# Reordering the projection steps of the later attention batches: begun half a unit sooner, the values' correction in two row tiles, the last diagonal ahead of its search

## The chip, the core and the metric

The kernel runs on one core of a Trainium2 chip, in float32. The core has four engines that compute: TensorE (PE; its weight loads are listed apart as PEld), VectorE (DVE), ScalarE (ACT) and GpSimd (POOL). SyncE (SP), ACT and POOL also issue DMA transfers between HBM and the on-chip SBUF. TensorE writes only into PSUM, whose eight banks are shared among the tiles below. The metric is device time in microseconds (us), the median of the runs shown; lower is better.

## The reference: what is computed

Eight batches of 1024 tokens with 512 features pass through a "macaron" block: half a feed-forward network, an attention, and half a feed-forward network again.

```python
x = x + 0.5 * ffn(layernorm(x))
x = x + attention(layernorm(x))
x = x + 0.5 * ffn(layernorm(x))
```

`ffn` is a mixture of 32 experts, each of which chooses tokens. A gate gives logits per token and expert, softmax runs over the tokens, and each expert takes its eight best tokens of a batch, merges them with their probabilities into one row, sends that row through a 512-2048-512 network with GELU, and adds the result back to the eight tokens. `attention` is a causal linear attention with 16 heads of 32 features: q = exp(x Wq + bq), k = exp(x Wk + bk), and

```python
kv  = cumsum(k[:, :, :, None] * v[:, :, None, :], axis=1)
k1  = cumsum(k, axis=1)
out = einsum('zsD,zsDd->zsd', q, kv) / sum(q * k1, -1)
```

## The kernel before

**Stages.** The kernel first routes all tokens, then runs the experts of the first FFN (`experts(0, ...)`), the attention, the experts of the second FFN, and a last scatter. The experts' weights are 268 MB in each FFN, so these stages stream weights. Beside the first FFN, TensorE has time to spare, and `speculate` uses it: for batches 4 to 7 it centres x, projects it to q, k and v (without the first FFN's contribution, which isn't known yet and has rank 32) and stores the result in HBM as `ahead_d`.

**Units and chunks.** The attention handles a batch as eight chunks `c` of 128 tokens; two chunks make a unit `u` (U = 2, UT = 256 columns). Each unit needs q, k, the running sum k1 of k, and the values `va`. For batches 0 to 3 `project` makes them with full matmuls. For batches 4 to 7 (`NB0 = 4`) `project_rest` loads `ahead_d` as `pre` and corrects it by rank 32, with `pm` (the routing probabilities) times `oW` (the experts' outputs times the weights). The tile `pm4` holds `pm` of the batch four times, once in each block of 32 partitions. The steps of `project_rest` are:

- L631: add the output bias to x on POOL. L636 to L650: spread the reciprocal deviations over the partitions (`rsb`), scale `pm` to `pmr` and scale the q and k part of `pre`, on POOL. Issue the load of the next unit's `pre` (L652). Then two bare yields.
- L663: eight correction matmuls for q and k (`ps_qk`), into both `sp` tiles. L672: two additions on DVE. L675: eight exps on ACT.
- L678: `sum_keys`, four scans on DVE (L709).
- L684: two matmuls for the values' correction (`ps_v`), both from the same 32 rows, each listed as two records. L688: two DVE steps that make `va`.
- L697: `times_keys`, qk = q * k1 on POOL (L720).

**A chunk of the attention.** `scores` (L766) multiplies k by q into the two `sp` tiles; DVE masks one half into `am` (L777), ACT copies the other (L782) and POOL masks it (L784). `denominators`, in the even chunk, sums q * k1 (`ps_den`, L728) and inverts it on DVE (`rd`, L736); `spread_denominators` repeats it (L747, L754). `turn_keys` transposes k (L816, copy L818). `attend` multiplies `am` by `va` (`ps_n`, L830), adds the state's part (L842), divides (`at`, L851) and updates the state (L862, L871). `project_out` multiplies by Wo (L880), adds to x (L887) and takes moments for the next routing (L314). The generator `begin` of the next batch (`begun`) scatters the first FFN's output into x (L293, L300, L308) and takes moments. The generator `route` (`gate`) makes the routing for the second FFN: the gate's scale (L380 to L399), `choose` (the searches L407, L412 and L414, the softmax L416 to L424), the diagonal `diag` (L512), `ps_pmT` (L519), `ps_m` (L539), `ps_mT` (L562).

**What sets the order.** `attention` is a loop over batches and chunks that calls these functions and advances the generators with `next`. The order of the calls is the program order. The instructions are then put in each engine's queue by the framework's planner: it plays the program with its own durations and gives each engine the ready instruction that comes first in program order, so the queue can differ from program order. An engine runs its queue in order. `tc.keep_in_program_order` pins an instruction behind the one before it on its engine. In an odd chunk of the kernel before, the order of calls is: a step of `begun`, `scores`, a step of `ahead` (the bare yield), `turn_keys`, `project_out` of the chunk before, a step of `ahead` (L656 to L697, all of it), a step of `gate`, `attend`. PSUM: `mm` has three banks in turn (`ps_o`, `ps_n`, `ps_v`, `ps_kt`, `ps_den`, `ps_sc` and others), `sp0` and `sp1` take two banks each and serve `scores`, `ps_qk` and the spread denominators in turn, and `sum` holds the state.

**The last routing.** For batch 7 `route` gets a tile `el` and runs without pauses behind the last chunk. Its scale is done in groups of 4, 2, 1 and 1 chunks. `choose` then pins the index search (L427) behind the reciprocal (L424), and `diag` (L512) follows both on DVE.

Of the kernel before, what the change touches and what calls it, by code (L numbers as in the profile page):

```python
# [8 lines left out]
F32 = mybir.dt.float32  # L9
# [6 lines left out]
P = 128  # L16
# [4 lines left out]
def kernel(  # L21
# [52 lines left out]
    nc = tc.nc  # L74
    B, S, D = x_in.shape
    E = w1.shape[0]
    FF = w1.shape[2]
    NCH = S // P
# [3 lines left out]
    U = 2  # L82
# [3 lines left out]
    NB0 = 4  # L86
# [285 lines left out]
    def gate_scale(t, s, b, lg, rs, at, k):  # L372


        own = slice(32 * (b % 4), 32 * (b % 4) + E)
        raw = s["raw", b]
        pr = t.mm.tile([NCH, P], F32, tag="mm", name=f"ps_rsT_{b}_{at}")
        nc.tensor.transpose(pr[:k, :], rs[:, at : at + k], ident)
        rsT = t.p2.tile([NCH, P], F32, tag="rsT", name=f"rsT_{b}_{at}")
        nc.scalar.copy(rsT[:k, :], pr[:k, :])  # L380
        yield
        halves = range(at // 4, (at + k - 1) // 4 + 1)
        c0, n = at % 4, min(k, 4)
        rows = slice(E * c0, E * (c0 + n))
        ps = t.mm.tile([P, 2, P], F32, tag="mm", name=f"ps_rs_{b}_{at}")
        for i, h in enumerate(halves):
            nc.tensor.matmul(
                ps[rows, h, :],
                lhsT=pick8[:k, i, :n, :].rearrange("k c e -> k (c e)"),
                rhs=rsT[:k, :],  # L390
                start=True,
                stop=True,
            )
        hs = slice(halves[0], halves[-1] + 1)
        nc.vector.tensor_mul(raw[rows, hs, :], raw[rows, hs, :], ps[rows, hs, :])
        to = lg.rearrange("p (h c s) -> p c h s", h=2, c=4)
        for c in range(c0, c0 + n):
            r = slice(E * c, E * (c + 1))
            nc.scalar.activation(  # L399
                to[own, c, hs, :], raw[r, hs, :], AF.Identity, bias=gb_sb[r]  # L400
            )

    def choose(t, lg, rows, g, name, listed=False, el=None):


        top = t.p2.tile([P, 8], F32, tag="top", name=f"top_{name}")
        nc.vector.max(top[rows, :], lg[rows, :])  # L407
        pinned = el is not None
        sm = t.p2.tile([P, 3], F32, tag="sm", name=f"sm_{name}")
        nc.vector.tensor_scalar_mul(sm[rows, 0:1], top[rows, 0:1], -1.0)  # L410
        rest = pm[:, g, :]
        nc.vector.match_replace(rest[rows, :], top[rows, :], lg[rows, :], -1.0e30)  # L412
        if listed and not pinned:
            nc.vector.max_index(chosen_idx[rows, g, :], top[rows, :], lg[rows, :])  # L414
        el = el if pinned else lg
        nc.scalar.activation(  # L416
            el[rows, :], lg[rows, :], AF.Exp, bias=sm[rows, 0:1], accum_out=sm[rows, 1:2]
        )
        kept = nc.vector.scalar_tensor_tensor(
            rest[rows, :], rest[rows, :], -0.9e30, el[rows, :], ALU.is_lt, ALU.mult  # L420
        )
        if pinned:
            tc.keep_in_program_order(kept)
        nc.vector.reciprocal(sm[rows, 2:3], sm[rows, 1:2])  # L424
        if pinned:
            tc.keep_in_program_order(
                nc.vector.max_index(chosen_idx[rows, g, :], top[rows, :], lg[rows, :])  # L427
            )
        return rest, sm[rows, 2:3]

    def gather_four(t, xs, rs4, chosen, r, g):
# [49 lines left out]
    def route(t, s, b, el=None):  # L481
# [25 lines left out]
                yield  # L507
        if el is None:
            yield
        chosen, r = choose(t, lg, rows, g, f"b{b}", True, el)  # L510
        diag = t.p2.tile([P, E], F32, tag="diag", name=f"diag_{b}")
        nc.vector.tensor_scalar_mul(diag[rows, :], ident[rows, rows], r)  # L512
        if el is None:
            yield

# [102 lines left out]

    def project_rest(t, s, b, u):

        xt, mv, rs = s["xt", b]
        pre = s.pop(("pre", b, u))
        if u == 0:
# [27 lines left out]
        if (b, u) < (B - 1, NCH // U - 1):  # L651
            load_ahead(t, s, *divmod(b * (NCH // U) + u + 1, NCH // U))  # L652
        yield
        yield

        qkT = open_unit(t, s, b, u)  # L656
        sp = [
# [15 lines left out]
        for n, bias in ((1, bk_sb), (0, bq_sb)):  # L673
            for oc in range(NDC):
                nc.scalar.activation(  # L675
                    qkT[:, oc, n, :], qkT[:, oc, n, :], AF.Exp, bias=bias[:, oc : oc + 1]
                )
        sum_keys(t, s, b, u)  # L678

        r = slice(32 * (b % 4), 32 * (b % 4) + E)  # L680
        for i in range(U):
            c = u * U + i
            ps = t.mm.tile([P, D], F32, tag="mm", name=f"ps_v_{b}_{c}")
            nc.tensor.matmul(  # L684
                ps, lhsT=pmr[r, i * P : (i + 1) * P], rhs=s["oWv"][r, :], start=True, stop=True
            )
            va = t.a2.tile([P, D], F32, tag="va", bufs=3, name=f"va_{b}_{c}")
            nc.vector.scalar_tensor_tensor(  # L688
                va,
                pre[:, (2 * NDC + i * 2) * UT : (2 * NDC + i * 2 + 2) * UT],  # L690
                rs[:, c : c + 1],
                ps,
                ALU.mult,
                ALU.add,
            )
            s["va", b, c] = va
        times_keys(t, s, b, u)  # L697
        yield

# [211 lines left out]
    def outputs_ahead(t, s):  # L911


        ocT = outputs_turned(t, s, NB0 // 4)
        s["oW"] = t.ow.tile([P, B - NB0, 2, P], F32, name="oW")
        for i in range(2):
            ps = t.mm.tile([P, 2, 2, P], F32, tag="mm", name=f"ps_oW{i}")
            for b in range(2):
                r = 32 * ((NB0 + 2 * i + b) % 4)
                for n, w in enumerate("qk"):  # L920
                    for dc in range(NDC):
                        for j in range(4):
                            nc.tensor.matmul(
                                ps[E * j : E * (j + 1), b, n, :],
                                lhsT=ocT[:, dc, r : r + E],
                                rhs=w_sb[w][:, dc, j * P : (j + 1) * P],
                                start=(dc == 0),
                                stop=(dc == NDC - 1),
                            )
            evacuate(s["oW"][:, 2 * i : 2 * i + 2], ps)  # L930
        s["oWv"] = t.ow.tile([P, D], F32, name="oWv")
        ps = t.mm.tile([P, D], F32, tag="mm", name="ps_oWv")
        for dc in range(NDC):
            nc.tensor.matmul(
                ps, lhsT=ocT[:, dc, :], rhs=w_sb["v"][:, dc, :], start=(dc == 0), stop=(dc == NDC - 1)
            )
        evacuate(s["oWv"], ps)

    def attention(t, early, preload):

# [46 lines left out]
        for b in range(B):  # L987
            for c in range(NCH):
                if c == 0:
# [12 lines left out]
                    if b + 1 < B:  # L1002
                        s["loaded", b + 1] = load_x(t.xp, x_in, b + 1, f"xt{(b + 1) % 3}")
                        begun = begin(b + 1)
                if c > 1:
                    next(begun, None)
                if b == B - 1 and c == 1:
                    preload(0)
                if b == B - 1 and c == NCH - 2:
                    late.close()  # L1010
                    preload(1)
                    preload(2)
                    preload(3)
                    el = end.enter_context(tc.tile_pool(name="el", bufs=1, side="right")).tile(
                        [P, S], F32, name="el"
                    )
                    gate = route(t, s, b, el)
                scores(t, s, b, c)
                if c % U == 0:
                    denominators(t, s, b, c // U)  # L1020
                    nb, nu = divmod(b * (NCH // U) + c // U + 1, NCH // U)
                    if (nb, nu) == (NB0, 0):

                        for i in range(2):
                            values(t, s, b, c + i)
                        early.close()
                        t.s1 = late.enter_context(
                            tc.tile_pool(name="s1", bufs=1, side="right", reuse_waits="tile")
                        )
                        t.s2 = late.enter_context(  # L1030
                            tc.tile_pool(name="s2", bufs=2, side="right", reuse_waits="tile")
                        )
                        load_ahead(t, s, nb, nu)
                    if (nb, nu) > (0, 1):
                        of = project if nb < NB0 else project_rest
                        ahead = of(t, s, nb, nu) if nb < B else iter(())
                        next(ahead, None)
                else:
                    next(ahead, None)
                if ("va", b, c) not in s:  # L1040
                    values(t, s, b, c)
                turn_keys(t, s, b, c)
                if last is not None:
                    project_out(t, s, *last)
                    if c == 0:
# [10 lines left out]
                if c % U == 0:  # L1056
                    spread_denominators(t, s, b, c // U)
                else:
                    next(ahead, None)
                next(gate, None)  # L1060
                if (b, c) == (0, 1):
                    outputs_turned(t, s, 0)
                attend(t, s, b, c)
                last = (b, c)
        gate_sums(t, s, B - 1, range(NCH - 2, NCH - 1))
        next(gate)
# [575 lines left out]
```

## Time and profile before

| what | value |
|---|---|
| median of 3 runs (lowest, highest) | 2618.5 us (2616.56, 2619.34) |
| the profiled execution: its time | 2614.58 us |
| its span, from the first to the last instruction | 2612.9 us |
| mean granted TensorE clock | 0.916 |
| busy in the span: PE, PEld, DVE, ACT, POOL | 2176.2, 1153.6, 869.7, 500.6, 376.8 us |
| HBM, mean over the span | 254 GB/s |
| attention: first and last scores of the trace | 859.7 and 1935.9 us |
| L631, of project_rest: first and last | 1398.8 and 1807.6 us |
| first matmul of the second FFN's experts (L1206) | 1971.59 us |

Durations and places in time come from the one profiled execution, counted from the start of its span. The page lists busy times for each engine; a line such as L663 is line 663 of the kernel. In a timeline a row gives start, duration, engine, line, operation, the tiles written and read, and how many instructions it merges; in brackets stands the idle time of the engine before it and what ended that. The row "PEclk" is the clock that TensorE was granted, in tenths.

### The profile page before, as it was taken

The page shows a single profiled execution, that of the slowest core. Times are in us where ns is not written, and L with a number is a line of the kernel's source. Part 1 is how long each engine was busy: PE and PEld are TensorE (multiplying, and loading weights), DVE is VectorE, ACT ScalarE, POOL GpSimd, SP SyncE. Part 2 cuts the span into 40 slices and gives each one's busy share as a digit, 9 for nine tenths or more (in the row PEclk, how much of TensorE's full clock was granted, in tenths as well). Part 3 has the DMA queues.
Part 4 walks back from the last instruction along what each step waited for, and adds up shares of the span by engine and source line. Part 5 has one row for each costly group of instructions (what it writes and reads, how often), then busy time and mean ns, then how long its engine had stood idle before and what let it go on. Part 6 is the DMA issues. An engine that isn't in the chain of part 4 may idle for free.

```text
span 2612.9 us, 41804 instructions
## 1 busy us (share of the span) xinstructions
PE 2176.2 (83%) x18679; PEld 1153.6 (44%) x18679; DVE 869.7 (33%) x1493; ACT 500.6 (19%) x967; POOL 376.8 (14%) x345
## 2 busy tenths in 40 slices
PE   8799999898977999999999989898886555555555
PEld 6354454454533666666666655555541111111111
DVE  7311111111102443544535476767751000100002
ACT  6300001000001322222222243343430000000000
POOL 0000000000000211111122244445324000000002
PEclk9899999999998999999999988999997778878788
DMA  7899999999996000010100323323159999999996
GB/s 278 316 417 428 426 427 427 427 427 427 428 429 234 1 18 11 11 50 19 59 2 19 95 81 132 112 107 108 66 196 377 422 428 428 428 428 427 428 428 255
DMA packets 95476, 667.97 MB, mean 256 GB/s; under 512 B 18222, under 2 KB 22574, under 8 KB 58432
## 3 DMA queue, kind: packets, MB, share of 16 engines
q1 hardware_dynamic: 73792, 621.45, 57.9%
q10 hardware_dynamic: 18432, 35.66, 3.5%
q0 software_dynamic: 3072, 8.19, 0.8%
q8 instruction: 146, 2.39, 0.4%
q14 instruction: 34, 0.28, 0.0%
HBM read 614.34 MB, written 48.23 MB: 254 GB/s over the span
## 4 chain that ended last, share of the span: by engine, by line
PE 49%; issue 23%; DMA 14%; DVE 7%; ACT 1%; POOL 1%; SPq 0%; POOLq 0%; ACTq 0%; DVEq 0%
DMA w<-in_w 10%; PE ps_o L880 8%; PE ps_k L599 4%; PE ps_q L599 4%; PE ps_v L800 4%; PE ps_sk L1116 3%; PE ps_sq L1116 3%; PE p_ps L1229 3%; PE h_ps L1206 3%; PE ps_sv L1133 2%; PE ps_n L830 2%; PE sp L766 2%; PE ps_n L842 2%; DMA xg<-out,chosen_idx 2%; DVE un L709 1%
## 5 line engine op out<-in xcount | busy, mean ns | idle before, releaser
L1206 PE MATMUL h_ps<-w,mT 128*8 128x512 f32 x2048 | 288.6, 698 | 126.7 <-DMA w<-in_w 126.0
L1215 DVE STREAM_TRANSPOSE hs<-h_ps 128x512 f32<-128x512 f32 x64 | 45.9, 717 | 723.7 <-PE h_ps L1206 723.7
L1229 PE MATMUL p_ps<-w,pm 128*32 128x512 f32 x1024 | 172.1, 805 | 132.8 <-DMA w<-in_w 127.8
L880 PE MATMUL ps_o<-wo_sb,at 128*128 128x512 f32 x512 | 236.4, 605 | 1.0 <-DVE at L851 0.8
L1206 PEld LDWEIGHTS h_ps<-w,mT 128*8 128x8 f32 x2048 | 50.4, 95 | 339.7 <-issue 205.0
L1229 PE MATMUL p_ps<-w,gl 128*32 128x512 f32 x1024 | 132.7, 651 | 40.7 <-DMA w<-in_w 40.4
L590 POOL TENSOR_TENSOR xt<-xt,bo_sb 128x512 f32<-128x512 f32 x32 | 45.8, 1447 | 767.0 <-PE ps_ocT L338 706.7
L1229 PEld LDWEIGHTS p_ps<-w,pm 128*32 128x32 f32 x1024 | 35.3, 129 | 270.4 <-issue 134.4
L880 PEld LDWEIGHTS ps_o<-wo_sb,at 128*128 128x128 f32 x512 | 94.1, 194 | 100.7 <-issue 95.9
L784 POOL TENSOR_SCALAR_AFFINE_SELECT am<-am 128x512 f32<-128x512 f32 x128 | 78.7, 639 | 413.7 <-ACT am L782 276.3
L314 DVE BATCH_NORM_STATS2 st<-xt 128x6 f32<-128x512 f32 x192 | 129.4, 686 | 4.1 <-DMA xt<-in_x 1.0
L599 PE MATMUL ps_k<-xnT,wk_sb 128*128 128x256 f32 x512 | 115.3, 383 | 10.8 <-ACT xnT L339 10.8
L1222 ACT ACTIVATE pm<-a 128x128 f32<-128x128 f32 x32 | 9.9, 309 | 586.5 <-DVE a L1217 586.5
L1116 PE MATMUL ps_sq<-xcT,wq_sb 128*128 128x256 f32 x512 | 118.3, 387 | 4.0 <-ACT xcT L241 4.0
L1116 PE MATMUL ps_sk<-xcT,wk_sb 128*128 128x256 f32 x512 | 117.3, 385 | 0.0
L1133 PE MATMUL ps_sv<-wv_sb,xcT 128*128 128x512 f32 x256 | 115.6, 599 | 0.0
L800 PE MATMUL ps_v<-wv_sb,xnT 128*128 128x512 f32 x256 | 115.1, 593 | 0.0
L599 PE MATMUL ps_q<-xnT,wq_sb 128*128 128x256 f32 x512 | 115.1, 382 | 0.0
L1116 PEld LDWEIGHTS ps_sq<-xcT,wq_sb 128*128 128x128 f32 x512 | 96.4, 192 | 34.8 <-issue 17.0
L1116 PEld LDWEIGHTS ps_sk<-xcT,wk_sb 128*128 128x128 f32 x512 | 96.7, 191 | 27.9 <-issue 15.4
L599 PEld LDWEIGHTS ps_k<-xnT,wk_sb 128*128 128x128 f32 x512 | 95.8, 190 | 28.4 <-ACT xnT L339 14.6
L766 PE MATMUL sp<-un 32*128 32x128 f32 x2048 | 100.1, 293 | 7.2 <-ACT un L675 7.0
(245 smaller groups left out, 2888.8 us busy)
## 6 DMA issues: line engine op xcount, KB each, us to landing
w<-in_w SPq DMA_DIRECT2D x256, 2048.0 KB, 29.5
xt<-in_x SPq DMA_DIRECT2D x31, 1024.0 KB, 10.7
pre<-ahead_d SPq DMA_DIRECT2D x16, 1536.0 KB, 6.7
ahead_d<-ahead_qk ACTq DMA_DIRECT2D x16, 1024.0 KB, 11.7
out<-xt SPq DMA_DIRECT2D x16, 1024.0 KB, 4.4
xs<-in_x ACTq DMA_DIRECT2D x16, 512.0 KB, 19.8
ahead_d<-ahead_v ACTq DMA_DIRECT2D x16, 512.0 KB, 11.1
pm<-pm SPq DMA_DIRECT2D x16, 128.0 KB, 2.5
```

The source lines that it names most:

```text
L314: nc.vector.bn_stats(st, xt[:, c, :])
L599: nc.tensor.matmul(ps[:, o, :], lhsT=w_sb[n][:, dc, oc * P : (oc + 1) * P], rhs=xnT[:, dc, :], start=(dc == 0), stop=(dc == NDC - 1),)
L766: nc.tensor.matmul(sp[r // 2][:, r % 2, og, :], lhsT=kT[hr, og, cols], rhs=qT[hr, og, cols], start=True, stop=True,)
L784: nc.gpsimd.affine_select(out=am[1][:, i, :, :], in_=am[1][:, i, :, :], pattern=[[0, NDC], [1, P]], compare_op=ALU.is_ge, fill=0.0, base=0 ...
L800: nc.tensor.matmul(ps, lhsT=s["xnT", b, c // U][:, dc, cols], rhs=w_sb["v"][:, dc, :], start=(dc == 0), stop=(dc == NDC - 1),)
L830: nc.tensor.matmul(ps[hr, og, :], lhsT=va[:, (og * HG + r) * HD : (og * HG + r + 1) * HD], rhs=am[r // 2][:, r % 2, og, :], start=(og == 0 ...
L842: nc.tensor.matmul(ps[hr, og, :], lhsT=kv[hr, og, :], rhs=qT[hr, og, cols], start=False, stop=True, skip_group_check=True,)
L880: nc.tensor.matmul(ps, lhsT=at[:, oc, :], rhs=w_sb["o"][:, oc, :], start=(oc == 0), stop=(oc == NDC - 1),)
L1116: nc.tensor.matmul(ps[:, o, :], lhsT=w_sb[w][:, dc, oc * P : (oc + 1) * P], rhs=xcT[:, dc, :], start=(dc == 0), stop=(dc == NDC - 1),)
L1133: nc.tensor.matmul(ps, lhsT=xcT[:, dc, i * P : (i + 1) * P], rhs=w_sb["v"][:, dc, :], start=(dc == 0), stop=(dc == NDC - 1),)
L1206: nc.tensor.matmul(h[32 * j : 32 * j + B, :], lhsT=mT[:, dc, e, :], rhs=w1h[dc // 2][:, dc % 2, j * 512 : (j + 1) * 512], start=(dc == 0), ...
L1229: nc.tensor.matmul(pp[32 * j : 32 * (j + 1), :], lhsT=gl4[e % 4][:, q, :, :].rearrange("p i b -> p (i b)"), rhs=w2h[q // (NU // 2)][:, q % ...
```

## The change

Six edits, all in the attention.

- `project_rest` is cut into four steps instead of three (one of them bare): (A) up to the next load; (B) `ps_qk`, additions, exps; (C) the values' correction and `va`; (D) `sum_keys` and `times_keys`.
- For units of batches 4 to 7 (`rest`) A still runs in the even chunk behind the denominators. B now runs at the end of the even chunk, behind `attend`. In the odd chunk `turn_keys`, C and a step of `gate` come ahead of `scores`; D comes behind `project_out` and behind the step of `begun`, which in these odd chunks moves there from the head of the chunk.
- The two value matmuls of a unit use two row tiles: chunk i uses the 32 rows of batch b + i (mod 4) of `pmr`, with a second copy of `oWv` that is turned by 32 partitions. That copy is made once, by two DMAs on SP, at the start of the later batches.
- In `choose` with `el`, the index search is no longer issued; `route` scales the diagonal first and then issues the search, both pinned in this order.
- In `gate_scale` the copy of `rsT` is on DVE instead of ACT where a single chunk is handled (`k == 1`, twice, in the last routing).

```diff
-        nc.scalar.copy(rsT[:k, :], pr[:k, :])
+        (nc.vector.tensor_copy if k == 1 else nc.scalar.copy)(rsT[:k, :], pr[:k, :])
...
         if pinned:
-            tc.keep_in_program_order(
-                nc.vector.max_index(chosen_idx[rows, g, :], top[rows, :], lg[rows, :])
-            )
+            return rest, sm[rows, 2:3], top
...
-        chosen, r = choose(t, lg, rows, g, f"b{b}", True, el)
+        chosen, r, *top = choose(t, lg, rows, g, f"b{b}", True, el)
         diag = t.p2.tile([P, E], F32, tag="diag", name=f"diag_{b}")
-        nc.vector.tensor_scalar_mul(diag[rows, :], ident[rows, rows], r)
+        scaled = nc.vector.tensor_scalar_mul(diag[rows, :], ident[rows, rows], r)
+        if el is not None:
+            tc.keep_in_program_order(scaled)
+            tc.keep_in_program_order(
+                nc.vector.max_index(chosen_idx[rows, g, :], top[0][rows, :], lg[rows, :])
+            )
...
             load_ahead(t, s, *divmod(b * (NCH // U) + u + 1, NCH // U))
-        yield
         yield
...
-        sum_keys(t, s, b, u)
-
-        r = slice(32 * (b % 4), 32 * (b % 4) + E)
+        yield
+
+        ps = [t.mm.tile([P, D], F32, tag="mm", name=f"ps_v_{b}_{u * U + i}") for i in range(U)]
+        for i in range(U):
+            r = slice(E * ((b + i) % 4), E * ((b + i) % 4 + 1))
+            nc.tensor.matmul(
+                ps[i],
+                lhsT=pmr[r, i * P : (i + 1) * P],
+                rhs=s["oWv", i][r, :],
+                start=True,
+                stop=True,
+            )
...
             s["va", b, c] = va
+        yield
+        sum_keys(t, s, b, u)
         times_keys(t, s, b, u)
         yield
...
+                nb, nu = divmod(b * (NCH // U) + c // U + 1, NCH // U)
+
+                rest = NB0 <= nb < B
-                if c > 1:
+                if c > 1 and not (rest and c % U):
                     next(begun, None)
...
+                if rest and c % U:
+                    turn_keys(t, s, b, c)
+                    next(ahead)
+                    next(gate, None)
                 scores(t, s, b, c)
...
+                        oWv = s["oWv", 1] = t.s1.tile([P, D], F32, name="oWv1")
+                        nc.sync.dma_start(oWv[E:], s["oWv", 0][: 3 * E])
+                        nc.sync.dma_start(oWv[:E], s["oWv", 0][3 * E :])
...
-                else:
+                elif not rest:
                     next(ahead, None)
...
-                turn_keys(t, s, b, c)
+                if not (rest and c % U):
+                    turn_keys(t, s, b, c)
...
                 else:
+                    if rest and c > 1:
+                        next(begun, None)
                     next(ahead, None)
-                next(gate, None)
+                if not (rest and c % U):
+                    next(gate, None)
...
                 attend(t, s, b, c)
+                if rest and c % U == 0:
+                    next(ahead)
                 last = (b, c)
```

More of the change, by code (lines that the diff above doesn't have):

```diff
@@ L677, in project_rest @@
                 )
-        sum_keys(t, s, b, u)
-        r = slice(32 * (b % 4), 32 * (b % 4) + E)
+        yield
[9 more added lines that the diff above has]
+            )
         for i in range(U):
             c = u * U + i
[L683 to L686, printed above, removed]
             va = t.a2.tile([P, D], F32, tag="va", bufs=3, name=f"va_{b}_{c}")
@@ L691, in project_rest @@
                 rs[:, c : c + 1],
-                ps,
+                ps[i],
                 ALU.mult,
@@ L930, in outputs_ahead @@
             evacuate(s["oW"][:, 2 * i : 2 * i + 2], ps)
-        s["oWv"] = t.ow.tile([P, D], F32, name="oWv")
+        s["oWv", 0] = t.ow.tile([P, D], F32, name="oWv")
         ps = t.mm.tile([P, D], F32, tag="mm", name="ps_oWv")
@@ L936, in outputs_ahead @@
             )
-        evacuate(s["oWv"], ps)
+        evacuate(s["oWv", 0], ps)
     def attention(t, early, preload):
@@ L1020, in attention @@
                     denominators(t, s, b, c // U)
-                    nb, nu = divmod(b * (NCH // U) + c // U + 1, NCH // U)
                     if (nb, nu) == (NB0, 0):
@@ L1033, in attention @@
                         load_ahead(t, s, nb, nu)
+                        oWv = s["oWv", 1] = t.s1.tile([P, D], F32, name="oWv1")
+                        nc.sync.dma_start(oWv[E:], s["oWv", 0][: 3 * E])
+                        nc.sync.dma_start(oWv[:E], s["oWv", 0][3 * E :])
                     if (nb, nu) > (0, 1):
-                        of = project if nb < NB0 else project_rest
+                        of = project_rest if rest else project
                         ahead = of(t, s, nb, nu) if nb < B else iter(())
                         next(ahead, None)
-                else:
+                elif not rest:
                     next(ahead, None)
```

## The prediction

> **What bounds the kernel now.** I read four views, from coarse to fine. First the page's slices, 65 us each (2612.9 / 40):
>
> ```profile
> PE   8799999898977999999999989898886555555555
> ...
> DVE  7311111111102443544535476767751000100002
> ...
> PEclk9899999999998999999999988999997778878788
> DMA  7899999999996000010100323323159999999996
> ```
>
> DMA is full in the two FFNs and nearly idle between them, in the attention (slices 13 to 29, about 820 to 1950 us). There TensorE is the fullest engine: 9 with a full clock in batches 0 to 3; from slice 22 (1437 us) on, where project_rest has taken away the big projection matmuls, 8s and 9s, with a clock of 8 and 9 in most slices and VectorE at 6 and 7. The change works in that stretch, so I cut it at the starts of batches 4 to 7 (the first scores, L766) in the stretches view. Behind the length stand the busy times, then the granted clock, the DMA share and GB/s:
>
> ```profile
> core 0: us, PE busy (x) PEld busy (x) DVE busy (x) ACT busy (x) POOL busy (x), PEclk, DMA share, GB/s
> 1513.00:1620.00 107.00, 97.93 (x1357) 60.82 (x1353) 77.92 (x116) 40.58 (x77) 50.78 (x42) 0.90 0.32 107
> 1620.00:1728.40 108.40, 97.08 (x1362) 60.02 (x1355) 78.90 (x121) 41.88 (x81) 50.53 (x40) 0.91 0.31 106
> 1728.40:1838.30 109.90, 97.81 (x1357) 58.81 (x1353) 80.64 (x121) 41.90 (x81) 50.46 (x40) 0.92 0.30 104
> 1838.30:1921.00 82.70, 72.26 (x1057) 44.66 (x1053) 55.51 (x80) 35.39 (x68) 30.33 (x24) 0.92 0.27 95
> ```
>
> Over these 408 us TensorE is idle for 9.1 + 11.3 + 12.1 + 10.4 = 42.9 us. The clock loses another busy x (1 - clock) = 9.8 + 8.7 + 7.8 + 5.8 = 32 us. So 75 us are to be won at most, with VectorE, at 79 us in a batch of 108, as the next floor. What the idle time waits for is in the waits of PE between 1513 and 1927 (total us, times, longest):
>
> ```profile
> PE ps_den L728 <- POOL qk L720: 14.8, 9, 2.8
> PE ps_n L830 <- DVE va L688: 13.1, 12, 2.0
> PE sp L766 <- ACT un L675: 7.0, 11, 1.0
> PE ps_rr L747 <- DVE rd L736: 5.1, 3, 2.2
> PE ps_kt L816 <- DVE at L851: 3.0, 3, 1.3
> ```
>
> The first three, 34.9 us, are waits for the results of project_rest. The timeline of chunk 7 of batch 4 shows how they arise:
>
> ```profile
> 1615.31 1.15 PE L663 MATMUL ps_qk<-pmr,oW 32*128 32x256 f32 x16
> ...
> 1616.28 1.88 PE L684 MATMUL ps_v<-oWv,pmr 32*128 32x512 f32 x4
> ...
> 1616.98 2.36 DVE L672 TENSOR_TENSOR un<-ps_qk,pre 128x1024 f32<-128x1024 f32 x2
> ...
> 1622.49 2.35 POOL L720 TENSOR_TENSOR qk<-un 128x1024 f32<-128x1024 f32 x1 [8.27 <-DVE un L709]
> ...
> 1624.89 1.08 PE L728 MATMUL ps_den<-qk,hsum 128*32 128x256 f32 x8 [2.79 <-POOL qk L720]
> ```
>
> One chain runs ps_qk (PE), two additions (DVE, 2.36), exps (ACT), four scans (DVE), the product (POOL, 2.35), den (PE). It starts only at 1615.31, behind the odd chunk's project_out, and den waits 2.79 us for its end. In chunks 1, 3 and 5 ps_n waits in the same way for va (L688), which queues on DVE behind the additions.
>
> **The change, part by part.** The instructions are issued in the order in which a planner finds them ready, with program order as priority, so an earlier place in the program moves a step only if its inputs are there. They are: pmr and the scaled pre come from POOL (L646, L650), done at 1609.3 in chunk 6, while ps_qk was issued at 1615.3. The sixteen units (batches 4 to 7) give these terms:
>
> (a) den. ps_qk, additions and exps come behind the even chunk's attend, some 5 us sooner (scores 1.17 and project_out 3.70 lie between). The longest wait is 2.8, so I count -13 of 14.8. Ends: 0 and -14.8.
>
> (b) va. Its matmuls and DVE steps now stand ahead of the odd chunk's scores; scores and project_out (4.9 us) lie between va and ps_n, where the longest wait was 2.0. -12 of 13.1. Ends: 0 and -13.1.
>
> (c) scores waiting for exp, all in chunks 3 and 4. The exps are sooner, but DVE was busy 22.28 of the 23.50 us from 1650.50 to 1674 (the routing's searches stand there), so half comes back as waits for DVE: -3.5 of 7.0. Ends: 0 and -7.
>
> (d) The waits for rd and at (5.1 + 3.0 + 0.8) come from that crowd and stay: 0.
>
> (e) The clock. Behind den's wait the stretches view shows
>
> ```profile
> 1616.40:1623.20 6.80, 5.51 (x104) 3.31 (x99) 6.77 (x11) 4.24 (x9) 0.71 (x1) 1.00 0.01 2
> 1623.20:1626.60 3.40, 1.71 (x11) 0.90 (x12) 2.07 (x3) 0.08 (x1) 2.81 (x3) 0.50 0.78 260
> ```
>
> the clock falls from 1.00 to 0.50, and 1626.6 to 1630 reads 0.50 too. (a) to (c) take away 28.5 of 42.9 us of idle time; other gaps of about 1 us left the clock alone, and one of 0.5 us stands before a fall, so I give half of the 32 us: -16. Ends: 0 and -32. [...]
>
> (f) The values' correction. Four records in one row tile take 1.88 us (1616.28). The same shape in two row tiles, ps_sc of L293 and L300, goes in pairs: starts at 1551.71 and 1552.25, the last 0.59 long, 1.13 together. 0.75 less in twelve units; in the four of chunk 3 the records already lie beside ps_pmT. -9. Ends: 0 and -16 x 0.94 = -15.
>
> (g) A new queue on ACT, POOL and the sp banks. ps_qk now holds both sp banks just ahead of the odd scores, which wait for both additions; project_out and turn_keys can fill that. Then scores' copy (L782) stands behind eight exps. Laid out from ps_qk's end: additions to 2.5, exps from 1.3 to 4.6 (3.3 in the timeline, 1618.24 to 1621.54), scores done about 3.1, copy (1.01) to 5.6, selects (1.22) to 6.8, ps_n. In the kernel before the copy follows at once. Behind the copy waits POOL's select, behind that ps_n. The delay of 1.5 us is covered by project_out (3.70) less copy and selects (2.2 and latencies), about 1.1; I take 0.7 a unit for what is over, with chunk 1's four gate activations (L399, 2.1 us) in that queue too: +11. Ends: 0 and 16 x 3.7 = 59 (nothing covers).
>
> (h) The last routing is the chain that starts FFN two. The rsT copy waits on ACT behind a table load (1952.01, 1.28 us) and junk, and ps_rs starts at 1953.70; on DVE the copy can start at 1952.55. No row has that copy on DVE; the nearest, L395 (0.28), gives ps_rs at 1952.9: -0.8. diag (1960.08) stands behind the search (L427, 0.06 + 1.21): -1.3; the search then lies beside ps_pmT (3.62 us on PE). Next late is that matmul group. The weight stream follows: it waits for the first h_ps matmuls (1971.59) to free a buffer, has a DMA share of 0.70 and 0.89 from 1960 to 1980, and is full from 1980 on. Whatever the attention gains also reaches the end this way. -2.1. Ends: 0 and -2.5.
>
> (i) Entry. Two DMAs are issued on SP behind pre and ahead of the four pm loads (2.90 us for four at 1491.57): pm lands up to 1.4 us later. But pmr ran at 1504.74 because POOL was at L650 until then. +0.5, ends 0 and 1.4. The pre load stays where it is; its buffer, freed by va, comes sooner. The moved begun (L308, L314) and gate steps have the same instructions as before: 0, with the DVE slack outside chunks 2 and 3 as cover; without it they cost what (c) and (d) show, 8.9 us.
>
> Sum: -13 - 12 - 3.5 - 16 - 9 + 11 - 2.1 + 0.5 = -44. The profiled execution took 2614.6 (span 2612.9), so 2570.5; the median shown lies 3.9 above it: **2574 us**, own range 2558 to 2592.
>
> **The rivals.**
> 1. The clock stays (half-clock follows strings of narrow matmuls, not gaps). For: 0.51 us of idle time at 1704.2, behind ps_mT and ps_kv, is followed by 3.4 us at 0.50. Against: the longest falls stand behind the longest gaps. (e) is 0: 2590. Chance 0.12. [...]
> 2. VectorE takes over: the additions and scans move, and va or at is late instead. For: 22.28 of 23.50 busy. Against: DVE is idle 30 us per batch elsewhere. Half of (a) and (b) returns with 8 us of clock: 2574 + 12.5 + 8 = 2595. Chance 0.11.
> 3. The planner moves little, since it already ranks by readiness; only (f) and (h) are left: 2607. Against: ps_qk was ready 6 us before it was issued. Chance 0.07.
> 4. Slower: (g) isn't covered. While scores wait for the sp banks, the planner sends project_out ahead; then copy, selects and ps_n have nothing over them, and each odd chunk stands for 1.5 + 1.01 + 1.22 = 3.7 us. The clock then stays low: -39 + 59 = +20, 2638. It decides from 39 / 16 = 2.4 us a unit. For: nothing is pinned. Against: attend's second half and the next scores can fill. Chance 0.16.
> 5. Better: (a) to (c) and (e) go whole, (g) is 0: -14.8 - 13.1 - 7 - 32 - 9 - 2.1 = -78: 2540. Chance 0.07.
> The forecast has 0.47.
>
> **Range and chances.** 2548 to 2624 leaves out most of rival 4 (0.13) and of rival 5 (0.05). About 0.2% (5 us) is what a measurement of this kernel can tell from no change. Faster by more: 0.46 + 0.12 + 0.10 + 0.07, 0.05 of rival 3 and 0.01 of rival 4, 0.81. Slower: 0.13 of rival 4. Between: 0.06.
>
> **What would show it.** Right: "ps_den <- POOL qk" and "ps_n <- DVE va" under 3 us together in the waits of PE; ps_v as pairs of 0.53; batches of 95 to 98 us; PEclk 0.95 in them; the search under ps_pmT. Rival 4: "ps_n <- POOL am" with 30 us or more. Rival 2: waits for at, rd or va as large as now. Rival 1: idle time gone, PEclk still 0.91. Wrong: batches still of 107 us, or lost time outside 1513 to 1975.

## The result, and the profile after

The changed kernel takes **2606.5 us** (median of 5 runs, 2605.33 to 2611.15), the kernel before 2617.9 us beside it (5 runs): a ratio of 0.9962, with a 95% interval of 0.9951 to 0.9973. The change saves 11 us where 44 were forecast: the sign was right, the size a quarter, and the time lies above the forecast's own range (2558 to 2592), inside the wide one. The profiled execution took 2606.22 us, with a span of 2604.5 us.

The slices of the changed kernel, 65 us each, answer to those of before:

```profile
PE   8799999898986999999999989999986565555555
...
PEclk9999999999998999999999989989888878777788
DMA  7799999999996000010100233333159999999995
```

TensorE's row has filled up in slices 24 to 28 (the later batches), but the clock's row has not risen there: 9, 9, 8, 9 and 8 stand in these slices, where 8, 9, 9, 9 and 9 stood before. The stretches view of batches 4 to 7 says the same (length, busy PE, PEld, DVE, ACT, POOL, then granted clock, DMA share, GB/s):

```profile
1518.00:1623.50 105.50, 98.19 (x1365) 58.08 (x1361) 77.75 (x120) 41.96 (x80) 51.34 (x42) 0.92 0.32 109
1623.50:1729.60 106.10, 99.45 (x1365) 59.82 (x1357) 77.23 (x120) 41.75 (x80) 50.30 (x40) 0.90 0.31 108
1729.60:1835.00 105.40, 98.05 (x1361) 57.45 (x1357) 77.72 (x120) 41.97 (x80) 50.31 (x40) 0.92 0.31 109
1835.00:1912.00 77.00, 72.76 (x989) 43.76 (x981) 52.28 (x75) 34.19 (x64) 30.26 (x24) 0.89 0.29 105
```

A batch takes 105 to 106 us, not the 95 to 98 that the prediction named, with TensorE busy for 93 to 94% of it and the clock at 0.90 to 0.92. The waits of PE between 1518 and 1915 (total, times, longest), cut to those that matter here:

```profile
PE ps_rs L388 <- DVE va L697: 5.2, 4, 1.3
PE ps_pmT L523 <- DVE va L697: 5.2, 4, 1.3
PE ps_mT L566 <- DVE va L697: 5.2, 4, 1.3
PE sp L777 <- DVE un L676: 3.5, 6, 0.6
...
PE ps_n L841 <- POOL am L795: 1.5, 8, 0.2
```

The two waits that the prediction wanted gone, den for the product and the attention for `va`, 27.9 us together, are not in the list any more. In their place the gate's matmuls (L388, L523, L566), which read nothing of `va`, wait 15.6 us for it. The timeline of chunk 1 of batch 5 shows why:

```profile
1634.16 1.15 PE L667 MATMUL ps_qk<-pmr,oW 32*128 32x256 f32 x16
...
1635.23 0.66 PE L827 MATMUL ps_kt<-ident,un 128*128 128x128 f32 x4
1635.39 2.36 DVE L676 TENSOR_TENSOR un<-ps_qk,pre 128x1024 f32<-128x1024 f32 x2 [0.34 <-PE ps_qk L667]
...
1635.82 1.13 PE L687 MATMUL ps_v<-oWv,pmr 32*128 32x512 f32 x4
...
1637.66 1.40 DVE L697 SCALAR_TENSOR_TENSOR va<-pre,rs,ps_v 128x512 f32<-128x512 f32 x2
...
1638.46 0.37 PE L388 MATMUL ps_rs<-rsT,pick 8*128 8x128 f32 x1 [1.30 <-DVE va L697]
...
1639.77 5.40 PE L891 MATMUL ps_o<-wo_sb,at 128*128 128x512 f32 x8
1640.19 0.56 ACT L829 COPY kc<-ps_kt 128x512 f32<-128x512 f32 x1
...
1642.39 2.36 POOL L731 TENSOR_TENSOR qk<-un 128x1024 f32<-128x1024 f32 x1 [9.53 <-ACT lg L400]
...
1644.69 1.23 POOL L795 TENSOR_SCALAR_AFFINE_SELECT am<-am 128x512 f32<-128x512 f32 x2
...
1645.97 1.06 PE L841 MATMUL ps_n<-am,va 128*32 128x128 f32 x26 [0.18 <-POOL am L795]
```

There are three `mm` banks. The turned keys hold one from 1635.23 until ScalarE copies them at 1640.19, behind all eight exps; the two `ps_v` hold the others until VectorE has made `va`, behind the two additions. The gate's `ps_rs` needs a fourth, and TensorE stands for 1.30 us; `project_out`, which the prediction had down as a filler, needs an `mm` bank as well. Further down, the two selects (L795) stand behind the product on POOL, though ScalarE's copy was done at 1643.64, and the attention's second part waits for them. The half clock, which lengthens `ps_o` from 3.70 to 5.40 us, covers most of that.

**Where the 8.4 us of the two profiled executions (2612.9 to 2604.5) come from.** I cut the span at VectorE's mask steps (L777 before, L788 after) and split the stretch from batch 4's first to batch 7's last in three: TensorE's idle time; the clock's loss, by estimate half of the busy time at half clock (`ps_o` records start 0.43 us apart at full clock and 0.85 at half, in both traces); and the rest, its work at full clock.

| stretch | before | after | difference | forecast |
|---|---|---|---|---|
| batches 4 to 7, idle | 45.4 | 25.6 | -19.8 | (a), (b), (c), (d), (g): -17.5 |
| the same, clock's loss | 31.4 | 35.8 | +4.4 | (e): -16 |
| the same, work | 344.5 | 345.5 | +1.0 | (f): -9 |
| entry: batch 3's chunk 6 to batch 4's chunk 0 | 31.2 | 36.9 | +5.7 | (i): +0.5 |
| last mask step to the second FFN's first product | 35.5 | 34.2 | -1.3 | (h): -2.1 |
| from there to the end | 641.3 | 643.8 | +2.5 | 0 |
| up to batch 3's chunk 6 | 1483.5 | 1482.8 | -0.7 | 0 |

The idle time fell by as much as forecast in sum. The clock, the work and the entry did not follow. Each column comes from one trace. Entry back, a run below whose code is the same from batch 4 on, has 30.5, 30.7 and 347.0 us in the first three rows, so differences of some 5 us there can be spread between executions.

### The profile page after: what moved, and what is told of

It reads as the page before. It is cut to its first block, busy times and chain, and to the rows that moved or that the text cites. A ratio compares the mean times of both kernels' runs of the same rounds, so it can differ in the third digit from the quotient of the medians.

```text
span 2604.5 us, 41783 instructions
## 1 busy us (share of the span) xinstructions
PE 2190.8 (84%) x18679; PEld 1153.6 (44%) x18679; DVE 862.3 (33%) x1495; ACT 500.4 (19%) x965; POOL 376.6 (14%) x345
## 4 chain that ended last, share of the span: by engine, by line
PE 50%; issue 23%; DMA 16%; DVE 5%; ACT 2%; POOL 1%; SPq 0%; POOLq 0%; ACTq 0%; DVEq 0%
DMA w<-in_w 11%; PE ps_o L891 8%; PE ps_k L603 4%; PE ps_q L603 4%; PE ps_v L811 4%; PE ps_sk L1143 3%; PE ps_sq L1143 3%; PE p_ps L1256 3%; PE h_ps L1233 3%; PE ps_n L841 2%; PE sp L777 2%; PE ps_n L853 2%; PE ps_sv L1160 2%; DMA xg<-out,chosen_idx 2%; PE ps_sc L293 1%
## 5 line engine op out<-in xcount | busy, mean ns | idle before, releaser
L1233 PE MATMUL h_ps<-w,mT 128*8 128x512 f32 x2048 | 294.4, 703 | 126.2 <-DMA w<-in_w 124.3
L891 PE MATMUL ps_o<-wo_sb,at 128*128 128x512 f32 x512 | 258.5, 652 | 0.2
L1233 PEld LDWEIGHTS h_ps<-w,mT 128*8 128x8 f32 x2048 | 51.2, 95 | 342.4 <-issue 208.7
L891 PEld LDWEIGHTS ps_o<-wo_sb,at 128*128 128x128 f32 x512 | 102.0, 210 | 115.0 <-issue 110.0
L795 POOL TENSOR_SCALAR_AFFINE_SELECT am<-am 128x512 f32<-128x512 f32 x128 | 79.0, 642 | 398.7 <-ACT am L793 260.8
L777 PE MATMUL sp<-un 32*128 32x128 f32 x2048 | 104.8, 302 | 3.9 <-DVE un L676 3.8
```

Of the source, the lines that this page charges most:

```text
L777: nc.tensor.matmul(sp[r // 2][:, r % 2, og, :], lhsT=kT[hr, og, cols], rhs=qT[hr, og, cols], start=True, stop=True,)
L795: nc.gpsimd.affine_select(out=am[1][:, i, :, :], in_=am[1][:, i, :, :], pattern=[[0, NDC], [1, P]], compare_op=ALU.is_ge, fill=0.0, base=0 ...
L891: nc.tensor.matmul(ps, lhsT=at[:, oc, :], rhs=w_sb["o"][:, oc, :], start=(oc == 0), stop=(oc == NDC - 1),)
L1233: nc.tensor.matmul(h[32 * j : 32 * j + B, :], lhsT=mT[:, dc, e, :], rhs=w1h[dc // 2][:, dc % 2, j * 512 : (j + 1) * 512], start=(dc == 0), ...
```

## The experiments

All ratios are to the kernel before, timed beside it on the same chip, with 95% intervals. The last three columns split the stretch of batches 4 to 7 as above, from one trace each.

| kernel | us | ratio | idle | clock | work |
|---|---|---|---|---|---|
| before | 2617.9 | 1 | 45.4 | 31.4 | 344.5 |
| after | 2606.5 | 0.9962 (0.9951 to 0.9973) | 25.6 | 35.8 | 345.5 |
| keys first | 2595.7 | 0.9923 (0.9899 to 0.9946) | 37.8 | 8.5 | 349.6 |
| gate back | 2608.3 | 0.9968 (0.9955 to 0.9982) | 32.7 | 17.9 | 355.5 |
| one row tile | 2609.0 | 0.9970 (0.9952 to 0.9987) | 17.5 | 29.0 | 356.0 |
| entry back | 2603.1 | 0.9950 (0.9935 to 0.9965) | 30.5 | 30.7 | 347.0 |
| wide | 2606.6 | 0.9968 (0.9956 to 0.9980) | 20.4 | 5.1 | 378.4 |
| narrow | 2628.8 | 1.0053 (1.0033 to 1.0073) | 14.6 | 41.0 | 369.4 |
| keys first and entry back | 2594.2 | 0.9917 (0.9902 to 0.9931) | 40.1 | 10.2 | 349.3 |
| the same, selects pinned | **2572.7** | 0.9827 (0.9810 to 0.9844) | 25.7 | 13.4 | 342.4 |
| before, tail alone | 2612.6 | 0.9995 (0.9982 to 1.0007) | 43.8 | 33.6 | 343.7 |
| before, rows alone | 2617.3 | 1.0009 (0.9996 to 1.0021) | 50.9 | 40.2 | 333.5 |
| after, selects pinned | 2596.0 | 0.9930 (0.9911 to 0.9948) | 25.8 | 28.9 | 342.3 |
| pinned, one row tile | 2576.1 | 0.9847 (0.9825 to 0.9868) | 18.8 | 13.7 | 347.5 |

### The held banks: keys first, gate back

Keys first turns the odd chunk's keys at the end of the even one, ahead of `ps_qk`, so that their bank is free when `ps_v` comes.

```diff
                 if rest and c % U:
-                    turn_keys(t, s, b, c)
                     next(ahead)
...
                 if rest and c % U == 0:
+                    turn_keys(t, s, b, c + 1)
                     next(ahead)
```

> The changed kernel, with one move: the odd chunk's turn_keys stands ahead of ps_qk instead of behind it. Theory A (PSUM banks): in each odd chunk with a gate step PE stands 1.30 us ahead of the gate's matmul because all three mm banks are held, one by ps_kt, whose copy queues on ACT behind eight exps, two by ps_v until va. With the keys turned first their copy comes ahead of the exps, a bank is free, and the twelve waits (15.6 us) go; the clock's falls behind them go in part: 12 to 25 us less than the changed kernel's 2606.5, so 2582 to 2595. Theory B (sp banks): PE would stand there anyway, because scores waits for the two additions on DVE that free sp; the waits change their name to scores behind the additions, 1.1 us each as in chunk 7 (0.51 + 0.64), and the time is 2603 to 2608.

Measured: 2595.7 us, just above the range of Theory A and far below that of Theory B. The gate's waits for `va` are gone, and with them most of the clock's loss, 35.8 to 8.5 us. But the idle time rose by 12 us. The waits of PE from 1515 to 1915 show a new one at the top:

```profile
PE ps_n L841 <- POOL am L795: 20.0, 28, 1.6
PE sp L777 <- DVE un L676: 10.2, 20, 0.6
```

Gate back puts the gate's step of the odd chunks behind `project_out` again, where it was before the change.

> The changed kernel, with the odd chunk's gate step back behind project_out and the step of sums, where it was in the kernel before. Theory A: no gate matmul stands ahead of scores any more, so the 15.6 us of waits for a bank go; scores waits for the additions instead (1.15 us in chunk 7), and the clock's falls stay: 2600 to 2607. Theory B: the same, with all of the wait back as scores behind the additions, 2604 to 2608. If the place of the gate step is itself what costs (ps_pmT lost its cover, ps_v: 9.7 us busy against 7.9), then 2596 to 2602.

Measured: 2608.3 us, no different from the changed kernel. The wait at the banks goes here too and the clock's loss halves, but the attention waits 11.7 us for the selects, the scores 10.7 us for the additions, and the work rises by 10 us: the busy time of `ps_n`'s group goes from 38.5 to 44.1 us and that of `ps_v` from 16.6 to 20.9. So the stop's going is not enough by itself. Keys first frees a bank as well and moves the four wide transposes of each odd chunk ahead of `ps_qk`; which of the two makes it 11 us faster, no run separates.

### The selects: keys first with pins, and pins alone

In keys first the product can start a microsecond before the scores' copy is done (product from 1638.26 to 1640.61, copy done at 1639.28, in batch 5's chunk 1). The planner puts it first, and the selects start at 1640.58. The pins hold POOL to program order, selects first. The pinned kernel ("the one before" is keys first and entry back, shown further down) has both of those edits as well:

```diff
-        nc.gpsimd.tensor_mul(qk, s["q", b, u], s["k1", b, u])
+        made = nc.gpsimd.tensor_mul(qk, s["q", b, u], s["k1", b, u])
+        if b >= NB0:
+            tc.keep_in_program_order(made)
...
-            nc.gpsimd.affine_select(
+            kept = nc.gpsimd.affine_select(
...
+            if c % U and b >= NB0:
+                tc.keep_in_program_order(kept)
```

> The one before, with GpSimd held to the program's order in the later batches: the odd chunk's two selects ahead of the product of queries and keys (2.36 us), behind which they stand in the keys-first run, where the attention waited 20 us for the selects in 28 waits. Theory: the product's place is the cause. Then this wait falls under 8 us, the product comes 1.2 us later and is not waited for (the denominators come some 4 us after it), and the time is 2575 to 2584. Rival: ScalarE's copy of the scores, behind the exponentials and the gate's line, is the later of the two inputs: then the wait stays over 14 us and the time within 4 us of the run before.

Measured: 2572.7 us, 21 less than without the pins, 1.7% below before, and 2 below the expected range. The waits of PE between 1511 and 1880:

```profile
PE sp L779 <- DVE un L676: 10.7, 21, 0.6
...
PE ps_den L741 <- POOL qk L731: 2.4, 1, 2.4
PE ps_n L845 <- POOL am L797: 2.4, 7, 0.6
```

The wait for the selects fell from 21.7 to 2.4 us, and den waits once for the product. The product's place was the cause; ScalarE's queue wasn't. Two of the pinned kernel's batches in the stretches view:

```profile
1614.10:1712.40 98.30, 92.09 (x1357) 55.48 (x1361) 77.17 (x120) 41.73 (x80) 50.79 (x40) 0.97 0.34 117
1712.40:1811.50 99.10, 92.06 (x1357) 55.26 (x1361) 77.70 (x121) 42.09 (x80) 50.78 (x40) 0.97 0.33 116
```

That is close to the stage that the prediction described (95 to 98 us, clock 0.95).

> The changed kernel with GpSimd's pins alone, the keys where the change has them. The wait of the attention for the selects is 1.5 us in the window of batches 4 to 7 there, the wait at the held banks 16 us. Theory: pins are worth something only once the banks are free, so within 4 us of the changed kernel: 2602 to 2608 us. Rival: the pins alone bring most of the 21 us that they bring on top of the keys: below 2595.

Measured: 2596.0 us. My theory here falls: the pins alone, with the banks held as before (the three waits for `va` are still 5.2 us each), bring some 8 us (0.9962 to 0.9930). The rival isn't met either, since 8 is less than half of 21. The 1.5 us that the waits of the changed kernel show were too small a measure: the busy time of the `ps_n` group falls too, as the groups of TensorE over batches 4 to 7 show (the changed kernel first; busy us and mean ns, then idle time before):

```profile
L841 PE MATMUL ps_n<-am,va 128*32 128x128 f32 x992 | 38.5, 276 | 1.5 <-POOL am L795 1.5
L845 PE MATMUL ps_n<-am,va 128*32 128x128 f32 x992 | 33.9, 275 | 0.0
```

In the timeline above, its first records stand from 1645.09 and the rest follow the select at 1645.97: part of that wait is booked as work. The other part of the gain is the clock's loss, 35.8 to 28.9; why that falls, no run shows, and it is little more than the spread between executions.

### What the clock follows: wide and narrow

Two useless matmuls of 512 columns stand ahead of the scores of each odd chunk of batches 4 to 7 and write into the banks that the scores then overwrite. They are pure extra work. The wide ones (shown) use all 128 by 128 cells, the narrow ones the first 32 rows and 32 columns of the same tiles; the order on every engine is the same in both kernels.

```diff
+        if c % U and b >= NB0:
+            for h in range(2):
+                nc.tensor.matmul(
+                    sp[h][:, 0, :, :],
+                    lhsT=ident,
+                    rhs=w_sb["o"][:, 0, :],
+                    start=True,
+                    stop=True,
+                )
```

> The changed kernel with two useless matmuls of 512 columns put ahead of the scores of every odd chunk of batches 4 to 7, into the banks that the scores overwrite; they fill all 128 by 128 cells of the array. Sixteen chunks with two of 0.43 us each are 14 us at most; part of it falls into the wait for the values' sum (1.3 us a chunk, three chunks in four). Theory that idle time decides the clock: they fill some idle time and no more, half clock of 17 to 20 us a batch stays or falls alike here and with the narrow ones, and the two times are the same. Theory that the array's activity in a window of 3.41 us decides (the share of cells times columns): the stretch of narrow matmuls ahead of each fall gets 0.1 to 0.13 more activity of a threshold near 0.15 to 0.18, so half clock falls below 10 us a batch, and the kernel is 8 to 20 us faster than with the narrow ones: 2598 to 2608 us against 2610 to 2620.

> The same as the wide one, instruction by instruction, but the two useless matmuls use 32 rows and 32 columns of the array: as many columns streamed, as much time on the engine, a sixteenth of the cells. Idle theory: as fast as the wide one, within 3 us. Activity theory: half clock as in the changed kernel (17 to 20 us a batch), 2610 to 2620 us.

Measured: 2606.6 and 2628.8 us. The wide kernel does some 33 us more work than the changed one (378.4 against 345.5) and takes as long, since its clock's loss is 5.1 instead of 35.8 us. (I had expected 14 us of extra work. A matmul of 512 columns is two records, and `ps_o`, four such matmuls, takes 3.70 us, so the 32 wide ones are 29.6.) The narrow one, which idles less (14.6 against 20.4 us), loses 41.0 us to the clock. That is the activity theory's side, though the narrow one's time lies above the 2610 to 2620 us expected of it. In the stretches view, two steps of 3.4 us of the narrow kernel (1671.3), and two of the wide one (1544.0):

```profile
1671.30:1674.70 3.40, 2.86 (x20) 1.95 (x18) 3.40 (x5) 3.40 (x9) 0.00 (x0) 1.00 0.11 22
1674.70:1678.10 3.40, 3.40 (x29) 1.68 (x32) 1.82 (x4) 0.52 (x2) 1.28 (x1) 0.50 0.89 318
```

```profile
1544.00:1547.40 3.40, 2.26 (x42) 1.57 (x36) 3.27 (x6) 1.44 (x4) 0.00 (x0) 1.00 0.01 2
1547.40:1550.80 3.40, 2.44 (x11) 1.59 (x12) 3.30 (x8) 0.96 (x2) 2.24 (x2) 1.00 0.00 0
```

In the narrow kernel TensorE is busy for 2.86 of 3.40 us, idle for 0.54 us, and the clock is halved behind it; in the wide one it is busy for 2.26 us, idle for 1.14, and the clock stays. By the measure in the last section, the first of these narrow windows used 0.06 of the array and the first of the wide ones 0.42. So idle time doesn't decide it in these windows; how much of the array works fits both.

### The two row tiles

One row tile gives the changed kernel the old correction again (both matmuls from the batch's own 32 rows, no turned copy); rows alone is the kernel before with the new correction and its copy.

```diff
-            r = slice(E * ((b + i) % 4), E * ((b + i) % 4 + 1))
+            r = slice(E * (b % 4), E * (b % 4 + 1))
...
-                rhs=s["oWv", i][r, :],
+                rhs=s["oWv", 0][r, :],
```

> The changed kernel, with both matmuls of the values' correction in one row tile again and without the second copy of oWv and its two DMAs. My term (f) said that two row tiles save 0.75 us a unit: one row tile would then cost 9 to 12 us, 2616 to 2619. The rival: behind ps_v PE waits for the additions or a bank until 2.4 us after ps_qk, so the shorter ps_v lies in front of a wait and saves nothing: 2605 to 2609, with ps_v 1.9 us long and the wait behind it shorter by 0.75.

> The kernel before with the values' correction by two row tiles alone (its copy of the weights too). The prediction's term: -9 us, 0.55 us a unit. Rival, from the run with one row tile in the changed kernel (no difference): what the pair saves lies ahead of a wait, here that of the attention for the values' sum or for its other inputs, and the time is within 3 us of before.

> The pinned kernel with the values' correction in one row tile, as before the change. The pair of 0.53 us becomes some 1.0 us, sixteen times. If the pair lies on TensorE's path in this kernel: 7 to 9 us slower, 2580 to 2582. If it lies ahead of the scores' wait for the additions (21 waits of 0.5 us, 10.7 us): that wait falls under 4 us and the time stays within 3 us of the pinned kernel.

Measured: 2609.0, 2617.3 and 2576.1 us, by the ratios 2, 2 and 5 us above the kernels that they vary, with intervals that overlap each time. The work does change, by 10.5 us in the changed kernel and 11.0 in the one before, a little more than the 9 of term (f), and by 5.1 in the pinned one. It comes back: with rows alone, idle time rises by 5.5 us (the waits for the product, for `va` and for the exps are 15.6, 19.5 and 9.9 us against 14.8, 13.1 and 7.0; that for `rd` falls from 5.1 to 0.7) and the clock's loss by 8.8. In the pinned kernel the wait of the scores for the additions falls from 10.7 to 5.7 us as the slower pair fills half of it: between the two expectations, nearer to the second.

### The entry and the tail

Entry back runs the first later unit, whose even chunk is still batch 3's, in the old order.

> The changed kernel, with the first unit of the later batches alone in the order of before: scores and project_out of batch 3's last chunk stand ahead of its ps_qk. My term (i) gave the entry 0.5 us. The trace says that ps_qk stands ahead of scores in PE's queue and waits 6.57 us for pmr, with 13.7 us of half clock from 1499.9 on; from batch 3's chunk 6 to batch 4's chunk 0 it takes 36.9 us against 31.2. If that is the cause, this run is 5 to 8 us faster than the changed kernel: 2598 to 2602. If the entry's loss comes from the two DMAs ahead of pm, which stay, it is 2604 to 2607.

Measured: 2603.1 us, between the two expectations. The entry took 30.8 instead of 36.9 us, but batch 4 took 108.8 instead of 105.5. In the changed kernel's timeline, POOL's line and TensorE's:

```profile
1503.71 0.72 POOL L651 TENSOR_TENSOR pmr<-pm,rsb 128x256 f32<-128x256 f32 x1 [0.48 <-DMA pm<-pm]
...
1504.49 2.09 PE L667 MATMUL ps_qk<-pmr,oW 32*128 32x256 f32 x16 [6.57 <-POOL pmr L651]
```

`ps_qk` now stands in TensorE's queue ahead of batch 3's last scores and a `project_out`, and waits 6.57 us for `pmr`, which comes behind 4.64 us of scaling on POOL and the load of `pm`. Before, those scores and that product were the work beside it.

> The changed kernel with the odd chunk's keys turned half a unit sooner, ahead of the products of queries and keys, and the first later unit (in batch 3) in the old order. Alone the two gave -10.8 and -3.4 us against the changed kernel. If they add: 2590 to 2594 us. Rival: the first unit's old order costs later batches again what it wins (the fourth batch was 3.3 us longer with it): 2594 to 2597.

Measured: 2594.2 us, at the border between the two expectations and within the interval of keys first alone. By the ratios the old entry is worth 1.5 to 3 us, with intervals that overlap, and not the 6 that its own stretch shows.

> The kernel before with the tail's edits alone (the last batch's small copy on VectorE, the diagonal ahead of its search). The prediction's term: -2.1 us. What the changed kernel's trace shows: the way from the last scores to the second FFN's first product shorter by 1.3 us, and the rest of the program longer by 2.5 us, as in every run with the new tail; if the edit is the cause of both: +1 us. If that rest has another cause: -1.3 us and an unchanged rest.

Measured: 2612.6 us, ratio 0.9995 (0.9982 to 1.0007): 1.3 us less, with an interval from 4.7 less to 1.8 more, so the forecast's 2.1 is neither shown nor excluded. Its trace shows the last stretch 0.7 us shorter. The rest behind it, 641.3 us before, is 642.9 here, 643.8 in the changed kernel, 641.7 with the pins alone and 647.5 in the pinned kernel, all four with the same code there. So most of the table's 2.5 us can be spread between runs. But from the last mask step to the end the two kernels with the old tail (before and rows alone) take 676.8 and 677.4 us, and the twelve with the new one 675.8 to 681.1. Whether the tail's gain reaches the end stays open; no trace shows that it does.

## Why the prediction was right in sign and wrong in size

**(a), (b), (c), (d), (g): the idle time.** Right in sum (-19.8 against -17.5), in part by luck, and not in its parts. Den's and `va`'s waits went wholly, as (a) and (b) said. Term (g) failed in its sentence that `project_out` and `turn_keys` can fill the wait for the additions: both need an `mm` bank, and the turned keys themselves kept the third one occupied. The price, 15.6 us, came near its 11 us by chance, since it was worked out for the copy and the selects.

**(e): the clock, -16.** This is the step that failed, by 20 us the largest miss: "(a) to (c) take away 28.5 of 42.9 us of idle time [...] so I give half of the 32 us". The idle time did go, by 19.8 us, and the clock's loss did not fall (31.4 us before, 35.8 after, 30.7 in entry back). The gap of 0.5 us ahead of a fall, which the prediction names in the same sentence, spoke against counting by idle time. Wide and narrow show what stands in its place: the clock is halved behind a window in which little of the array works, whether it idles or runs narrow matmuls (by the measure in the last section, behind all 67 windows under 0.25). The matmuls put ahead of the scores took the loss from 35.8 to 5.1 us where they were wide, and to 41.0 where they were narrow, so I take it that a wait's going helps the clock if wide work moves into its window. The gate's stop of 1.3 us lay amid narrow work, `ps_v` ahead of it and the scores behind; with the keys first the loss falls to 8.5 us, and with the stop gone but the keys where they were (gate back) to 17.9. Rival 1 had the right reason (strings of narrow matmuls) and came nearest in this term with its (e) of 0. Rival 3's 2607 us came nearest in the time, by luck: the planner did move the steps, as the 27.9 us of waits that went show. The narrow kernel, whose longest wait of TensorE between 1515 and 1910 is 0.9 us, loses 41.0 us to the clock: the runs bear out the rival's reason, and no long gap was needed.

**(f): the row tiles, -9.** Right as work (11.0 us less with the rows alone, 10.5 more in the changed kernel without them), wrong as time: it was counted as if every saving on a busy engine reached the end. The runs with the rows alone and without them show no difference in time. The pair saves narrow work in front of a wait: with one row tile in the changed kernel, the gate's matmuls wait 7.6 us for `va` instead of 15.6.

**(i): the entry, +0.5.** The prediction priced the two DMAs and missed that `ps_qk`, moved ahead, takes its place in TensorE's queue before its input is there, and what stands behind it waits those 6.57 us too. The stretch cost 5.7 us, of which the times show 1.5 to 3, not clear of their intervals.

**(h): the tail.** The steps came as described (the copy took 0.28 us, the search runs under `ps_pmT`); 1.3 of 2.1 us in the trace up to the second FFN's first product, too little for the times to tell, and not seen at the end.

**Rival 4** named the next limit: copy and selects late for `ps_n`. It showed in full only when the banks' wait was gone, with 20.0 us; its cause was POOL's order, not ScalarE's queue. With keys, pins and entry together the kernel takes 2572.7 us, near the 2574 forecast; but that is another kernel, and the forecast isn't made right by it.

Three losses lay over one another: the stop at the banks and much of the half clock went together, and the half clock's longer `ps_o` had covered the late selects. Keys first (some 10 us), pins (some 8) and the entry (some 3) add up to 22 us below the changed kernel if taken alone; together they give some 35 (0.9962 to 0.9827).

## What to carry to other kernels

Before moving a step forward, count the PSUM banks that it holds and until when, and ask whether each instruction meant as a filler can get one (here three held banks cost 15.6 us of waiting). Price the clock by what runs in each window, wide or narrow (5.1 and 41.0 us lost here), not by idle time. When a wait goes, look for the one that it covered: here it stood in another engine's queue, and pinning the product and the selects brought 21 us.

## What the hardware did that I had not expected

- **The clock's windows.** In the traces of before and after the granted clock is 1.00 or 0.50, and 153 of each trace's 154 stretches at one clock last a whole multiple of 3.41 us. Over batches 4 to 7 of the 14 kernels (1649 whole windows) I worked out, from the matmul records, how much of the array each window used: each record's share of the 128 by 128 cells times the columns that it streamed, with `ps_o` records back to back (one of 512 columns every 0.43 us) as 1. Of the windows that ran at full clock, all 67 under 0.25 were followed by half clock, and none of the 1219 above 0.40; between, both occur (83 of 156). The threshold of 0.15 to 0.18 in the expectation for wide was my estimate, on half this scale (two records of 0.43 us in 3.41 are 0.25 here, 0.1 to 0.13 there): 0.30 to 0.36 here, within the range where both occur, so no run shows a sharp threshold. Of the windows in which TensorE was busy throughout, 38 were followed by half clock; of the 216 in which it was busy for under 80%, 100 were followed by full. In the narrow kernel TensorE idles for 14.6 us over batches 4 to 7 and loses 41.0 to the clock, in the wide one for 20.4 and loses 5.1: busy time is not what the clock follows.
- **Useless work for nothing.** Sixteen pairs of wide matmuls, some 33 us more of work, cost no time that the runs could tell (ratios to before of 0.9968 and 0.9962, with intervals that overlap).
- **Waits booked as work.** A `ps_n` group whose second input was late showed 0.18 us of idle time and some 0.7 us more of busy time (1.94 us over both parts, idle time included, against 1.08 in a chunk with the selects first).
